# A hybrid of selective scans, additive attention and a graph-gated mixture of experts on one core: norms and keys placed beside other work, a second PSUM place for scores, a larger share for early experts, and gathers paced by small tiles

## The chip, the cores and the metric

One core of one Trainium2 chip runs the whole program in one launch. The metric is the device time in microseconds; below, "us" always means microseconds. Engines are called by their names in the profile: PE (TensorE), PEld (its weight loads), DVE (VectorE), ACT (ScalarE), POOL (GpSimd) and SP (SyncE, which issues nearly all DMAs).

## The reference

The input is `x` of 4 batches x 32 variables x 96 steps x 256 channels. Cut to what matters:

```python
# layer 0: group norm, then two Mamba blocks, one along time, one along the variables
x = x + L0(group_norm(x, 32 groups))
#   in each: xz = x @ in_w.T; depthwise conv of 4 taps; silu; dt, B, C = ...; softplus(dt)
#   h[t] = exp(dt[t] * A) * h[t-1] + dt[t] * B[t] * u[t]     16 states, 512 channels
#   y = (h . C + u * D) * silu(z);  out = y @ out_w.T
# layer 1: t = tokens of x, 4 x 3072 x 256
q, k = ln(t) @ Wt, ln(t) @ Wx                      # 32 features
e = tanh(q[:, :, None] + k[:, None, :] + bh) @ Wa  # every pair of tokens of a batch
t = t + softmax(e) @ ln(t)
# graph attention over 1,048,576 edges (src beyond the 12,288 tokens is clipped, such dst dropped), gives gates
alpha = softmax over the edges of a node of leaky_relu(a_src[src] + a_dst[dst])
scores = layernorm(sum alpha * h[src]).mean(heads);  gates = softmax(top 2 of 4)
t = t + sum over experts of gates * (gelu(ln(t) @ W1[e] + b1[e]) @ W2[e] + b2[e])
```

The tanh of every pair is the largest single piece: 4 x 3072 x 3072 x 32 values.

## The kernel before

The program is written as generators that hand out work in small steps; the order in which they are drawn is the order in which PE, ACT, DVE and POOL execute. Only SP's order is left to the scheduler.

**Layer 0** (`Layer0`) works in 64 blocks of 384 tokens: for each batch eight along time ("t") and eight along the variables ("d"), with the first time block of the next batch ahead of the "d" blocks. A block is 48 slots long; in it `back` runs the scan: decays `dA` on ACT (L385), inputs `dB` (L393) and scans `h` (L402) on DVE, products with `C` on POOL (L409). The rows `bB` and `bC` are broadcast by DMAs of 384 KB, two pairs ahead (L350). `front` prepares the next block (slots 9 to 45). It holds a wide tile with tag `uab`, one buffer, from slot 32. Up to block 16 sums over states are PE products (`lead`), afterwards POOL sums. The group norm of all four batches (`group_norm`, L120 to L132) comes before everything else: per batch and channel half, two loads of 768 KB, six `bn_stats`, then two small PE products that average over the channels of a group, and a root.

**Attention** (`Attention.units`) handles one "column" per round: one ACT tanh of 128 x 3072 (L815), 768 columns a batch. `scores` multiplies it into `pe` in PSUM (L788), eight columns a unit. After the eighth, `unit_tail` takes the maximum on DVE (L877), the exponential on ACT (L884), turns it round (L891) and multiplies by the values (L900). `th` has three buffers, `pe` a single one of two banks, so the products of a unit's first column are held until the exponential of the unit before is under way. Each round advances layer 0 by one slot.

What attention needs beforehand, the norm and projections of a batch (`keys`, some 48 steps), lies in the list `side`; `beside()` draws one step of it per round that has room. If the keys of a batch are missing when its first column is due, rounds go by without a tanh, one step of the keys in each.

**When layer 0 is done**, `Edges.sort` (DVE) compacts the edge lists beside the columns, with a budget of 2.4 us a column; its one-hot products go to PE. When the next-to-last batch is normalised, `Experts.early` computes experts of the finished tokens beside the last batch, as far as a budget allows that grows by `SLOT_US` a column; hidden products `ph` (L1632) are emptied by DVE (L1671), outputs `po` (L1640) also (L1683), and kept in DRAM. POOL fetches the destination rows of edges (`gd`, L1052).

**The tail** (`tail`) is an order written by slots: three slots an expert unit (block of 512 tokens, expert). `some(t)` gives POOL credit of `RATE` gathers a call and has it first read a token (`pace`, L1047) from the tile just computed, either a hidden tile of ACT (`h`, L1714) or an output of DVE (`ko`, L1704). Source rows `gs` (L1337) have four buffers. Group j of twelve edges a partition is scored at slot `G0 + PART*j//2`, spread by DVE (`rh`, L1378) and placed by PE (`pa`, L1388). When a quarter of the edges is placed, its gates are made and the kept outputs of its six blocks are added (L1717) and stored. `ps_h` and `ps_o` rotate by one counter over two pools each.

Of the kernel before, what the change touches and what calls it, by code (L numbers as in the profile page):

```python
# [26 lines left out]
P = 128  # L27
# [8 lines left out]
T = 384  # L36
# [26 lines left out]
FIRST, RATE = 14, 2.75  # L63
G0, PART = 10, 6
KO_BUFS = 2
SLOT_US, PRODUCT_US = 1.2, 0.11
# [8 lines left out]
class Layer0:  # L75
# [8 lines left out]
    def __init__(self, ctx, tc, ident, a, x1):  # L84
# [12 lines left out]
        self.group_norm()  # L97

    def group_norm(self):

        nc, wk, ps, const = self.nc, self.wk, self.ps, self.const
        gavg = const.tile([P, P], F32, tag="gavg", name="gavg")
        nc.sync.dma_start(gavg, self.a["gavg"])
        eps = const.tile([P, 1], F32, tag="eps", name="eps")
        nc.vector.memset(eps, 1e-5)
        self.gm = const.tile([P, KC, B], F32, tag="gm", name="gm")
        self.gr = const.tile([P, KC, B], F32, tag="gr", name="gr")
        HB = TOK // 2
        NB = HB // 512
        for b in range(B):  # L110
            gm = self.gm[:, :, b]
            mv = wk.tile([P, KC, 2], F32, tag="gmv", name="gmv")
            gv = wk.tile([P, KC], F32, tag="gv", name="gv")
            for k in range(KC):
                stats = wk.tile([P, 2, NB, 6], F32, tag="gst", name="gst")
                for i in range(2):
                    xs = wk.tile([P, HB], F32, tag="dt", name="xs", bufs=2)
                    nc.sync.dma_start(xs, self.a["xT"][k * P:(k + 1) * P, b, i * HB:(i + 1) * HB])
                    for j in range(NB):
                        nc.vector.bn_stats(stats[:, i, j, :], xs[:, j * 512:(j + 1) * 512])  # L120
                nc.vector.bn_aggr(mv[:, k, :], stats.rearrange("p i n s -> p (i n s)"))
            pg = ps.tile([P, T], F32, tag="pp", name="pg")
            nc.tensor.matmul(pg[:, :KC], gavg, mv[:, :, 0], start=True, stop=True)
            nc.vector.tensor_copy(gm, pg[:, :KC])

            nc.vector.tensor_tensor(gv, mv[:, :, 0], gm, ALU.subtract)
            nc.vector.tensor_tensor(gv, gv, gv, ALU.mult)
            nc.vector.tensor_tensor(gv, gv, mv[:, :, 1], ALU.add)
            pg2 = ps.tile([P, T], F32, tag="pp", name="pg2")
            nc.tensor.matmul(pg2[:, :KC], gavg, gv, start=True, stop=True)  # L130
            nc.scalar.activation(self.gr[:, :, b], pg2[:, :KC], AF.Sqrt, bias=eps)
        nc.vector.reciprocal(self.gr, self.gr)  # L132
# [419 lines left out]
    def run(self):  # L552
# [34 lines left out]
        for n, blk in enumerate(blocks):  # L587
# [15 lines left out]
            ahead = self.front(then, blk["lead"]) if then and not breaks else {}  # L603
            for slot in range(48):
# [3 lines left out]
                for part in (left[1], jobs[1], ending, ahead):  # L608
# [31 lines left out]
class Attention:  # L640
# [4 lines left out]
    def __init__(self, ctx, tc, ident, a, x1, x2, xn2T, tab_s, tab_a):  # L645
# [7 lines left out]
        self.ps_e = pool("ate", PE_BUFS, space=PSUM)  # L653
# [122 lines left out]
    def units(self, side):  # L776
# [24 lines left out]
        while i < B * PER + LAG or todo or self.later:  # L801
            b, col = self.entry, self.col = divmod(i, PER)
            if b < B and "krep" not in self.state[b]:
# [3 lines left out]
                for f in late:  # L807
                    f()
                yield
# [15 lines left out]
            if behind and i >= LAG:  # L825
                n, k = divmod(i - LAG, NK)
                if k == 0:

                    pe = self.ps_e.tile([P, 2, JB], F32, tag="pe", name="pe")
# [16 lines left out]
            elif todo and hasattr(todo[0], "us"):  # L846
                if not todo[0].full:
                    beside()
                todo.pop(0)()
# [12 lines left out]
            if busy is None:  # L862
                beside()
            i += 1
# [708 lines left out]
class Experts:  # L1573
# [3 lines left out]
    def __init__(self, ctx, tc, x2, xn2T, gates, out, dram, beside=None):  # L1577
# [4 lines left out]
        self.ps_h, self.ps_o = [pool("fp", 2, space=PSUM)], [pool("fo", 1, space=PSUM)]  # L1582
        self.kept, self.done = (beside.kept, beside.units()) if beside else ({}, [])
        self.xts, self.turn = {}, 0

    def open(self, ctx, w):
# [4 lines left out]
        self.ps_h.append(pool("fp2", 2, space=PSUM))  # L1591
        self.ps_o.append(pool("fo2", 1, space=PSUM))

    def bank(self, pools, shape, tag):
        self.turn += 1
        return pools[self.turn % len(pools)].tile(shape, F32, tag=tag, name=tag)
# [133 lines left out]
def tail(tc, a, ed, ex, w, tab_s, tab_a, gates):  # L1730


    with ExitStack() as ctx:
# [376 lines left out]
```

## Time and profile before

| | us |
|---|---|
| median of 3 runs (15323.25 to 15328.89) | 15326.61 |
| the profiled execution's own time | 15328.57 |
| its span, first to last instruction | 15326.8 |
| PE busy | 11744.9 (77%) |
| DVE busy | 11006.6 (72%) |
| ACT busy | 12153.9 (79%) |
| POOL busy | 8997.6 (59%) |
| tanh, L815: 3072 x 2848 ns | 8661.7 |

A share of busy time is an average over stages with different limits; the slices and a table of stretches tell them apart. The first tanh starts at 2565.3 us, the last at 14201.7; all before is layer 0 alone, all after is the tail. A matmul's end is modelled, so a busy PE isn't PE at its peak; the mean granted clock was 0.893.

### The profile page before, as it was taken

The numbers are of one execution on the slowest core, as the hardware profiler recorded it, in microseconds if no ns is written. First come the engines' busy times: TensorE is split into PE (matmuls) and PEld (weight loads), VectorE is DVE, ScalarE is ACT, GpSimd is POOL, SyncE is SP. The second block draws the span as 40 slices with busy tenths as digits, with TensorE's granted clock in tenths as the row PEclk, the third lists the DMA queues.
The fourth block names the chain that finished last, engine by engine and source line by source line (L and its number), as shares of the span: only waits on it lengthen the run. The fifth ranks groups of instructions, "written<-read, shape, count | busy, mean of one in ns | idle before, by whom it ended". The sixth has DMA issues, their size and how long they took to land. (4 is left out here: it accounts for less than half of the span.)

```text
span 15326.8 us, 225317 instructions
## 1 busy us (share of the span) xinstructions
PE 11744.9 (77%) x86496; PEld 5137.0 (34%) x86496; DVE 11006.6 (72%) x15895; ACT 12153.9 (79%) x9327; POOL 8997.6 (59%) x6935
## 2 busy tenths in 40 slices
PE   5666764777777767788887777888876778988997
PEld 2222332222222233333333333333332334433554
DVE  7888888777777887777777877577778864321367
ACT  3443334999999979999999899999997889999221
POOL 4555556777777767767767677477750024400684
PEclk8888887888888888989998889999988989999998
DMA  5666665445445444454454444355531000010234
GB/s 192 204 203 200 198 204 167 149 148 156 152 150 151 158 156 148 150 152 151 151 150 156 147 149 152 110 156 151 154 127 37 24 13 13 10 31 22 66 95 138
DMA packets 1209121, 2007.93 MB, mean 131 GB/s; under 512 B 412384, under 2 KB 655712, under 8 KB 1204960
## 3 DMA queue, kind: packets, MB, share of 16 engines
q1 hardware_dynamic: 1180384, 1988.07, 41.6%
q0 software_dynamic: 27648, 5.36, 0.8%
q8 instruction: 680, 11.14, 0.3%
q14 instruction: 409, 3.35, 0.1%
HBM read 1875.19 MB, written 117.83 MB: 130 GB/s over the span
## 5 line engine op out<-in xcount | busy, mean ns | idle before, releaser
L815 ACT ACTIVATE th<-krep,qsel 128x3072 f32<-128x3072 f32 x3072 | 8661.7, 2848 | 411.1 <-PE pe L788 392.0
L788 PE MATMUL pe<-th,wa_blk 128*32 128x384 f32 x49152 | 4999.3, 535 | 1196.7 <-ACT pr L884 957.3
L409 POOL TENSOR_TENSOR h<-h,bC 128x768 f32<-128x768 f32 x2048 | 3756.2, 1834 | 3000.4 <-DVE h L402 2634.4
L402 DVE TENSOR_TENSOR_SCAN h<-dA,dB 128x384 f32<-128x384 f32 x4096 | 3687.3, 942 | 1109.4 <-ACT dA L385 752.9
L788 PEld LDWEIGHTS pe<-th,wa_blk 128*32 128x32 f32 x49152 | 1448.0, 116 | 3775.6 <-issue 1992.1
L393 DVE TENSOR_TENSOR dB<-bB,dtu 128x768 f32<-128x768 f32 x2048 | 1942.3, 948 | 123.3 <-DMA bB<-bc 91.2
L385 ACT ACTIVATE dA<-dt,t_A 128x380 f32<-128x380 f32 x2048 | 1127.1, 571 | 887.6 <-DVE h L402 883.1
L385 ACT ACTIVATE dA<-dt,d_A 128x372 f32<-128x372 f32 x2048 | 1102.9, 562 | 601.3 <-DVE h L402 595.9
L428 PE MATMUL py<-h,ident 128*128 128x384 f32 x2176 | 1010.1, 597 | 679.6 <-POOL h L409 678.2
L416 POOL TENSOR_TENSOR h<-h 128x768 f32<-128x768 f32 x752 | 1423.0, 1892 | 53.6
L900 PE MATMUL pv<-xn,pT 128*32 128x257 f32 x18432 | 1116.1, 391 | 172.3 <-DVE pT L893 171.4
L959 POOL TENSOR_SCALAR sf<-sel,f 128x32 f32<-128x32 f32 x384 | 148.6, 410 | 1641.6 <-ACT f L955 1533.9
L893 DVE COPY pT<-ptw 128x512 f32<-128x512 f32 (+1 forms) x768 | 419.0, 546 | 703.7 <-PE ptw L891 703.0
L428 PEld LDWEIGHTS py<-h,ident 128*128 128x128 f32 x2176 | 445.4, 223 | 1247.6 <-POOL h L409 1015.2
L900 PEld LDWEIGHTS pv<-xn,pT 128*32 128x32 f32 x18432 | 583.5, 112 | 759.7 <-DVE pT L893 317.4
L417 POOL TENSOR_TENSOR h<-h 128x384 f32<-128x384 f32 x752 | 783.7, 1042 | 59.0
L418 POOL TENSOR_TENSOR y<-y,h 128x384 f32<-128x384 f32 x752 | 779.9, 1037 | 59.0
L1714 ACT ACTIVATE h<-ph,b 128x512 f32<-128x512 f32 x148 | 96.7, 685 | 662.9 <-POOL pace L1047 473.9
L1337 POOL DMA_INDIRECT gs<-tab_s,si x432 | 526.6, 1219 | 131.3 <-issue 98.8
L891 PE MATMUL ptw<-ident,pr 128*128 128x128 f32 x2304 | 484.7, 328 | 143.5 <-DVE pT L893 79.6
L902 DVE COPY pvs<-pv 128x257 f32<-128x257 f32 x384 | 160.2, 417 | 569.0 <-PE pv L900 568.8
L1052 POOL DMA_INDIRECT gd<-tab_a,di x432 | 467.2, 1082 | 140.6 <-issue 133.4
(302 smaller groups left out, 15311.0 us busy)
## 6 DMA issues: line engine op xcount, KB each, us to landing
bB<-bc SPq DMA_DIRECT2D x2048, 384.0 KB
bC<-bc SPq DMA_DIRECT2D x2048, 384.0 KB
all<-kept SPq DMA_DIRECT2D x24, 2048.0 KB
x<-x SPq DMA_DIRECT2D x144, 256.0 KB
kept<-ko SPq DMA_DIRECT2D x59, 512.0 KB
x<-x SPq DMA_DIRECT2D x192, 128.0 KB
xt<-xn2T SPq DMA_DIRECT2D x41, 512.0 KB
qsel<-xn2T SPq DMA_DIRECT2D x75, 256.0 KB
```

The source lines that it names most:

```text
L385: nc.scalar.activation(inner(dA[:, :T]), inner(blk["dt"][:, e, :]), AF.Exp, scale=blk["w"]["A"][:, e, i + s:i + s + 1])
L393: nc.vector.tensor_tensor(dB, blk["bB"].pop(j), z["dtu"].unsqueeze(1).to_broadcast([P, SB, T]), ALU.mult)
L402: nc.vector.tensor_tensor_scan(h[:, s, :], z.pop(("dA", e, i + s))[:, :T], z["dB"][:, s, :], 0.0, ALU.mult, ALU.add)
L409: nc.gpsimd.tensor_tensor(h, h, blk["bC"].pop(j), ALU.mult)
L416: nc.gpsimd.tensor_tensor(h0, h0, h1, ALU.add)
L417: nc.gpsimd.tensor_tensor(h0[:, 0, :], h0[:, 0, :], h0[:, 1, :], ALU.add)
L418: nc.gpsimd.tensor_tensor(y[e], y[e], h0[:, 0, :], ALU.add)
L428: nc.tensor.matmul(z["py"], self.ident, h[:, s, :], start=(i == 0), stop=(i == DS - 1))
L788: nc.tensor.matmul(pe[q * QU:(q + 1) * QU, j, :KQ // 2], self.wa[:, k, :], th[:, c0:c0 + KQ // 2], start=(k == 0), stop=(k == NK - 1))
L815: nc.scalar.activation(th, s["krep"], AF.Tanh, bias=s["qsel"][:, col:col + 1])
L900: nc.tensor.matmul(pv[q * QU:(q + 1) * QU, :C + 1], pT[:, i, q * QU:(q + 1) * QU], s["xn"][:, q * NK + i, :], start=(i == 0), stop=(i == N ...
L1337: nc.gpsimd.indirect_dma_start(out=gs[:, u, :], out_offset=None, in_=rows, in_offset=bass.IndirectOffsetOnAxis(ap=ed.si[:, q, c0 + u:c0 + ...
```

## The change

1. `group_norm(0)` alone stays at the start. The nine remaining steps (two channel halves and the factors, for batches 1 to 3) are handed out by `norm_beside` to blocks 1, 2, 3 and 17 to 22, in the slots 0 to 23. Their data stand in the wide tile, both halves at once.
2. In rounds without keys two steps of `side` are drawn instead of one; likewise in rounds with room, as long as layer 0 is a batch ahead (`asked > b + 1`).
3. When layer 0 is done, a second pool gives a second place for `pe`; units alternate, and nothing is held. For it `ph` of the early experts has one bank instead of two.
4. `SLOT_US` 1.2 to 1.35: 29 early expert units instead of 22, so 30 in the tail instead of 37 (counted in the two programs).
5. In the tail `some` copies a token into a small tile (eight buffers), by ACT after a hidden tile, or sets one to zero on DVE after an output; POOL reads that. `RATE` 2.75 to 3.2, `PART` 6 to 5: 176 tokens are read instead of 209.
6. `bank` counts per tag. The tail has for `ph` one bank and three, for `po` one and one.

```diff
-FIRST, RATE = 14, 2.75
-G0, PART = 10, 6
+FIRST, RATE = 14, 3.2
+G0, PART = 10, 5
-SLOT_US, PRODUCT_US = 1.2, 0.11
+SLOT_US, PRODUCT_US = 1.35, 0.11
...
-        self.group_norm()
+        self.norm_constants()
+        self.group_norm(0)
+        self.norms = [(b, k) for b in range(1, B) for k in range(KC + 1)]
...
+        def load():
+            v["x"] = self.wide("xs")
+            v["st"] = self.wk.tile([P, NB, 6], F32, tag="gst", name="gst")
+            for h in range(2):
+                cols = slice(h * TOK // 2, (h + 1) * TOK // 2)
+                nc.sync.dma_start(v["x"][:, cols], self.a["xT"][k * P:(k + 1) * P, b, cols])
...
+    def norm_beside(self):
+        if not self.norms:
+            return {}
+        b, k = self.norms.pop(0)
+        if k == KC:
+            mean, variance, mean2, root = self.factors(b)
+            return {0: [mean], 1: [variance], 12: [mean2, root]}
+        return {slot: [f] for slot, f in zip((0, 10, 12, 14, 17, 20, 23), self.channel_norm(b, k))}
...
+            norms = self.norm_beside() if n in (1, 2, 3) or n > 2 * NBLK else {}
...
-                for part in (left[1], jobs[1], ending, ahead):
+                for part in (left[1], jobs[1], ending, ahead, norms):
...
+                beside()
                 yield
                 beside()
                 continue
...
-                    pe = self.ps_e.tile([P, 2, JB], F32, tag="pe", name="pe")
+                    places = self.ps_e2 if self.ps_e2 and n // NK % 2 else self.ps_e
+                    pe = places.tile([P, 2, JB], F32, tag="pe", name="pe")
+                if k == 0 and not self.ps_e2:
                     held = behind.pop(0)
...
                     beside()
+                    if self.asked > b + 1:
+                        beside()
...
             if busy is None:
                 beside()
+                if self.asked > b + 1:
+                    beside()
...
-        self.ps_h, self.ps_o = [pool("fp", 2, space=PSUM)], [pool("fo", 1, space=PSUM)]
+        self.ps_h, self.ps_o = [pool("fp", 1, space=PSUM)], [pool("fo", 1, space=PSUM)]
...
-        self.ps_h.append(pool("fp2", 2, space=PSUM))
+        self.ps_h += [pool("fp2", 3, space=PSUM)] * 3
...
     def bank(self, pools, shape, tag):
-        self.turn += 1
-        return pools[self.turn % len(pools)].tile(shape, F32, tag=tag, name=tag)
+        self.turn[tag] = self.turn.get(tag, -1) + 1
+        return pools[self.turn[tag] % len(pools)].tile(shape, F32, tag=tag, name=tag)
...
             credit[0] += RATE
             if credit[0] >= 1:
-                ed.behind(t)
+                tok = gr.wk.tile([P, QU], F32, tag="tok", name="tok", bufs=8)
+                if t is None:
+                    nc.vector.memset(tok, 0.0)
+                else:
+                    nc.scalar.copy(tok, t)
+                ed.behind(tok)
...
-                some(to[n - 1][:, 2 * part - 1, :QU])
+                some()
...
+                att.ps_e2 = actx.enter_context(
+                    tc.tile_pool(name="ate2", bufs=1, side="right", space=PSUM))
```

## The prediction

> **What bounds the kernel now.** I read four views in this order: the page's 40 slices (stages), the table of stretches cut at the stage borders, the waits of one stretch, and the groups of GpSimd in the last one. A slice is 383 us.
>
> ```profile
> PE   5666764777777767788887777888876778988997
> DVE  7888888777777887777777877577778864321367
> ACT  3443334999999979999999899999997889999221
> POOL 4555556777777767767767677477750024400684
> ```
>
> The reader sees three regimes: up to slice 6 ACT is at 3 or 4 and DVE at 8 (layer 0 alone); then ACT at 9 up to slice 37, with dips at 15, 23 and 31 to 33; then the tail, PE and POOL.
>
> ```profile
> core 0: us, PE busy (x) PEld busy (x) DVE busy (x) ACT busy (x) POOL busy (x), PEclk, DMA share, GB/s
> 0.00:62.00 62.00, 4.60 (x16) 4.00 (x16) 36.26 (x83) 3.88 (x7) 0.19 (x4) 1.00 0.79 254
> 62.00:2390.00 2328.00, 1532.86 (x3376) 680.42 (x3376) 1963.82 (x2366) 933.85 (x1637) 1354.55 (x856) 0.85 0.63 200
> 2390.00:2557.00 167.00, 77.09 (x187) 44.28 (x186) 141.46 (x238) 41.87 (x68) 110.33 (x77) 0.64 0.53 164
> 2557.00:5230.00 2673.00, 1977.89 (x17276) 749.89 (x17275) 2078.72 (x2787) 2626.81 (x1987) 2019.72 (x1441) 0.88 0.49 151
> 5490.00:5575.00 85.00, 48.41 (x126) 29.61 (x127) 74.89 (x121) 20.87 (x34) 56.81 (x39) 0.66 0.50 159
> 11760.00:12470.00 710.00, 533.59 (x4768) 211.65 (x4768) 632.98 (x1036) 583.30 (x242) 24.61 (x29) 0.89 0.09 28
> 12470.00:14203.00 1733.00, 1539.17 (x15844) 704.19 (x15840) 545.41 (x1054) 1691.27 (x697) 476.31 (x716) 0.95 0.08 18
> 14286.00:15165.00 879.00, 811.75 (x2403) 468.10 (x2402) 520.69 (x925) 194.74 (x250) 739.47 (x734) 0.96 0.33 85
> ```
>
> In the first 62 us only the group norm runs. In 2390:2557 and 5490:5575 ACT is 25% busy: attention waits for keys, and VectorE (85%, 88%) is what works. In 2557:5230 and 12470:14203 ACT is 98% busy: bound. In 11760:12470 ACT falls to 82% while DVE, sorting edges, is at 89%. In the tail's main stretch PE (92%) and POOL (84%) are both near full.
>
> ```profile
> ACT th L815 <- PE pe L788: 75.9, 47, 6.7
> PE pe L788 <- ACT pr L884: 77.7, 18, 10.3
> ACT pr L884 <- DVE nb L877: 41.5, 13, 7.6
> PE po L1640 <- DVE ko L1683: 25.7, 9, 7.3
> ```
>
> These are waits of 11760:12470: the one score place in PSUM makes PE wait for the exponential, the tanh waits for PE, and the exponential for DVE's maximum.
>
> ```profile
> L1337 POOL DMA_INDIRECT gs<-tab_s,si x422 | 517.1, 1225 | 106.6 <-issue 96.1 <-DVE y L1717 2.3 <-ACT h L1714 1.9
> L1052 POOL DMA_INDIRECT gd<-tab_a,di x104 | 116.8, 1123 | 27.9 <-issue 27.9
> L1047 POOL TENSOR_SCALAR pace<-h 128x32 f32<-128x32 f32 x140 | 66.6, 476 | 3.6
> L1047 POOL TENSOR_SCALAR pace<-ko 128x32 f32<-128x32 f32 x68 | 39.8, 586 | 1.6
> ```
>
> All of POOL in 14286:15165: its idle time is almost only "issue", 0.19 us an instruction. So POOL is full there, and ACT's 473.9 us of waiting for `pace` in the tail is the echo of that.
>
> [...] the trace has 1.283 us loads [...] so 1.28 is used. [...] `gs`, 0.94 us at the shortest and 2.96 while a 2.16 us `rh` of DVE runs; so POOL's mean of 1.2 should stay.
>
> **The parts.** Two counts from the instruction order of both programs (no time is in it): the first tanh comes after 1136 decays instead of 1168, and at the border of batches 0 and 1 8 decays stand between tanhs instead of 26. At four decays in three slots that is 24 and 13.5 slots less without a tanh.
>
> *Norms.* Removed at the start: three of four batches. `gr` is ready at 60.2 now; with batch 0 alone (second channel now waits for the one wide place: statistics end at 10.2, load about 4, six statistics 3.8, two small products and root 3.5) at about 22: -38. Added to blocks 1 to 3: 12 bn_stats x 0.63 + 2 aggregates x 0.32 + small ones = 9 us of DVE, which is at 84% in 62:2390 and sets the pace: +9. Four loads of 768 KB stand in SP's queue ahead of `bB`, `bC`; at the 254 GB/s of the start each is 3.1 us, and the broadcasts are two pairs ahead: +0 to +12, I take 3. Batches 2 and 3 fall in blocks 17 to 22: +6 where keys are made with DVE as bound, else beside an ACT that is full. Three root table loads: +4, counted below. Sum -20 (-38 to 0).
>
> *Keys.* A slot of layer 0 alone is (2190 - 105)/(16 x 48) = 2.7 us; in the keys' stall 208/48 = 4.3. The keys' own work stays, so 24 slots fewer give 24 x 2.9 = -70 (none if waits within a keys step set the 4.3; -104 at full price). Border 0/1: now 48 columns and 19.5 stalled slots from request to next tanh, 283 us; after, 24 and 6, with two steps each, at some 5.5 us: 165. That is -118, but 24 columns at 3.8 had to be done before: +91. So -97 when batch 1 begins. Layer 0 is then 37 slots behind the columns: as many columns run beside it at 3.95 us (mean of batch 2) instead of at 3.01 (1733/576): +35. Sum -62 (-90 to 0). Who is late next: VectorE, at each later border, in fewer columns.
>
> *Second PSUM place against one bank for `ph`.* In 11390:12470 th<-pe costs ACT 60.5 + 75.9 = 136 us; the second place takes away its cause. What it can give is limited by DVE: 633 + 285 busy of 1080, and 2.7 more expert units in these columns add 2.7 x (4 x 0.74 + 2 x 0.68) = 12. Against it, PE now waits at each `ph` for DVE. Nearest row: `po`, with one bank all along, 25.7 us for 12 evictions, 2.1 each; about 42 evictions x 2.1 = 88 us on a PE that is 75% busy and no longer loses its 158 us to `pr`. I take -35 (-100 to +40). In 12470:14203 ACT's th<-pe is 35: -20 at best. Added there: seven more gelus at 1.9 = 13 and 8 + 6 table loads = 18, all on the bound: +31. PE gets 4.6 units x 16.7 = 77 us more, 89% to 93%, and some 70 `ph` waits of 0.4 (po<-ko here: 9.5 us in 23) to 1: +10. Sum of this stage +21 (-10 to +70).
>
> *Tail.* Seven units leave it: 7 x 15 us of PE (ph 273.9 + po 280.9 over 37). But POOL has the same 526 gathers from 14286 on: 526 x 1.205 + 176 tokens x 0.512 + 702 x 0.19 = 857, against 879. So -22, not -105. The units' 119 ACT copies (0.2 us, as the 128x4 exponential) lie on an ACT that is 22% busy; 57 memsets (0.06) on DVE wait for a token place eight back, where DVE now waits for POOL 6.9 us in all: ol, rh, additions and so PE stand behind it: +7. RATE and PART bring more gathers a slot (POOL sooner full) and fewer slots; from POOL's last gather to the last `pa` it is 13 slots instead of 14. Closing blocks unchanged (81 us). Sum -15 (-90 to +20).
>
> Together -20 - 62 - 35 + 21 - 15 = -111. The profiled execution is 15328.6 (span 15326.8), 2 above the median of the three runs: 15328.6 - 111 = 15217.6, so about **15216** as a median.
>
> **Rivals.** *The tail follows PE.* PE at 92% speaks for it; if POOL gets room, the tail gives -105 instead of -15: 15126. *Denser keys buy nothing*: DVE is 85% busy in the stall, slots grow in proportion, the stall lasts as long; -62 becomes 0: 15278. *Slower: the lone `ph` bank.* If each of some 110 evictions holds PE behind the sort's instructions and tanh follows PE, the experts' larger share makes PE the bound from 11760 on: the second place gives nothing (0 for -35), 110 x 2.1 = 231 come instead of 21: 15216 + 35 + 210 = 15461. With the second place giving nothing, the gain is gone at (111 - 35 + 21)/110 = 0.9 us an eviction that reaches ACT, and above 1.2 the kernel is slower. Against it: three th buffers and 158 us of PE wait that go away. *The places do not alternate*, or `ph` serializes before them: H stays as it is, 15250.
>
> **How the numbers follow.** Forecast 0.60, tail by PE 0.16, keys nothing 0.14, `ph` bound 0.10 (a part of it under the full price). Errors of the parts together are about 85 around 15216; the range 15110 to 15310 leaves out most of the last rival and a little at the lower end. About 0.2% (31 us) is what a measurement of this kernel can tell from no change. Faster by more: nearly all of the first two, most of the third: 0.85. Same 0.06, slower 0.09.
>
> **What would show it.** Right: first decay at about 70 instead of 105; first tanh some 100 us sooner; next border's gap near 30 us instead of 85; no PE pe <- ACT pr in the last batch; some PE ph <- DVE h; POOL still without idle time in the tail, ending some 20 us sooner by its own length. Wrong: POOL idle in the tail (PE bound, larger gain); a last batch with more than 3.1 us a column (`ph`); bB waits in blocks 1 and 2 of more than 12 us.

## The result: slower by 60 us, where a gain of 111 had been forecast

| | before | after |
|---|---|---|
| median of 6 runs each, us | 15325.19 (15322.06 to 15328.89) | 15384.85 (15371.01 to 15396.19) |
| ratio, with its 95% interval | | 1.0037 [1.0027, 1.0048] |
| profiled execution, us (span) | 15328.57 (15326.8) | 15383.73 (15381.5) |

The forecast was 15216, and its range ended at 15310. Landmarks below are read from the traces, each of a single execution; where the medians say more, they are given. The page of the changed kernel has these slices:

```profile
PE   5666765677777767888888677888876779988886
DVE  8888887777777777777777877577767873332367
ACT  3443436999999979999999799999996879999221
POOL 5555556777777657767777577476750014410684
```

The stages have kept their places. ACT's dip at the second border is still there (slice 23), and DVE is at 7 and 8 in slices 31 to 33, where edges are sorted. The table of stretches of the changed kernel, with the columns of the table shown before:

```profile
0.00:26.00 26.00, 3.63 (x8) 2.18 (x8) 10.87 (x30) 3.09 (x4) 0.19 (x4) 1.00 0.78 242
26.00:2356.00 2330.00, 1515.09 (x3369) 673.26 (x3368) 1966.93 (x2379) 934.58 (x1634) 1347.82 (x852) 0.86 0.63 201
2356.00:2477.00 121.00, 65.13 (x176) 40.02 (x176) 92.17 (x187) 21.11 (x36) 54.08 (x37) 0.70 0.42 133
2477.00:5163.00 2686.00, 2003.04 (x17268) 755.72 (x17268) 2097.53 (x2792) 2634.81 (x1986) 2005.79 (x1435) 0.86 0.49 151
5465.00:5517.00 52.00, 29.73 (x90) 17.10 (x94) 34.84 (x67) 9.67 (x14) 20.95 (x15) 0.61 0.35 114
11741.00:12695.00 954.00, 733.76 (x6576) 306.66 (x6576) 785.30 (x1242) 782.26 (x323) 64.89 (x91) 0.91 0.09 29
12695.00:14250.00 1555.00, 1402.59 (x14342) 662.13 (x14338) 510.64 (x984) 1516.10 (x629) 434.57 (x654) 0.97 0.09 22
14330.00:15218.00 888.00, 775.78 (x2243) 435.74 (x2244) 531.22 (x985) 214.71 (x358) 730.69 (x700) 0.94 0.31 80
```

The group norm's start has shrunk (first row), the keys' stall is 121 us where it was 167, and the gap where batch 1 begins is 52 where it was 85. So the first third gained. In 11741:12695, the columns 2304 to 2560, ACT and DVE are both at 82%. The same columns of the kernel before:

```profile
11761.00:12660.00 899.00, 704.03 (x6566) 293.34 (x6566) 695.30 (x1153) 766.83 (x316) 117.09 (x165) 0.90 0.08 24
```

There ACT was at 85% and DVE at 77%. DVE does 90 us more in these columns now, and it is the sort: its instructions take 636 us there instead of 540. Layer 0's last decay came 90 us later (at 11467.9 instead of 11378.1 us), the sort begins only when layer 0 is done, and so more of it falls into these columns.

To see where the gain went, each piece between two landmarks (starts of layer 0's first decay and of the columns' tanhs) is compared:

| stretch | before, us | after, us | difference |
|---|---|---|---|
| start to first decay | 105.2 | 67.3 | -38 |
| first decay to first tanh | 2460.1 | 2410.0 | -50 |
| first tanh to column 768 (batch 1) | 3008.7 | 3039.9 | +31 |
| 768 to 1408 | 2596.7 | 2560.1 | -37 |
| 1408 to 1536 (keys of batch 2) | 543.6 | 578.8 | +35 |
| 1536 to 2304 | 3046.7 | 3084.6 | +38 |
| 2304 to 2560 (edges sorted) | 899.4 | 954.7 | +55 |
| 2560 to last tanh, 3071 | 1541.3 | 1554.3 | +13 |
| last tanh to end | 1125.1 | 1131.8 | +7 |

The sum is +55 (rounded terms give 54). 88 us are saved up to the first tanh, and 143 net come back behind it. Landmarks of runs with identical code up to there differ by up to 26 us (the run with tokens, whose code differs in the tail alone, stood 14 us ahead at the first tanh and 24 at the last). Their stretches behind the first tanh agree within about 10 us, so the difference of a stretch is worth more than one landmark.

The waits of 11741:12695 in the changed kernel (us in total, times, longest):

```profile
ACT th L860 <- PE pe L832: 113.7, 71, 7.1
PE ph L1684 <- DVE h L1723: 68.1, 36, 11.5
PE pe L832 <- ACT pr L936: 52.5, 16, 9.6
ACT pr L936 <- DVE nb L929: 40.8, 19, 9.2
PE po L1692 <- DVE ko L1735: 28.9, 11, 8.6
```

`pe` still waits for `pr`, which two alternating places should have ended, and the wait for the one `ph` bank is new: 1.9 us for each of 36. GpSimd's groups in 14330:15218 of the changed kernel:

```profile
L1389 POOL DMA_INDIRECT gs<-tab_s,si x420 | 528.3, 1258 | 109.4 <-issue 105.7 <-DVE tok L1817 1.7 <-DVE oh L1426 0.6
L1104 POOL DMA_INDIRECT gd<-tab_a,di x104 | 126.7, 1218 | 28.2 <-issue 27.9 <-ACT h L1766 0.3
L1099 POOL TENSOR_SCALAR pace<-tok 128x32 f32<-128x32 f32 x175 | 77.8, 445 | 14.2 <-ACT h L1766 9.9
```

POOL is as full as before: busy for 82% of this stretch (84% before), and 133.6 us of its idle time are "issue". It reads 33 tokens fewer, but each gather takes longer (1258 and 1218 ns against 1225 and 1123).

### The profile page after: what moved, and what is told of

Same layout as the page of the kernel before. It is cut to its first block, busy times and chain, and to the rows that moved or that the text cites. A ratio compares the mean times of both kernels' runs of the same rounds, so it can differ in the third digit from the quotient of the medians.

```text
span 15381.5 us, 225571 instructions
## 1 busy us (share of the span) xinstructions
PE 11765.2 (76%) x86496; PEld 5132.3 (33%) x86496; DVE 11066.4 (72%) x15983; ACT 12192.1 (79%) x9436; POOL 8977.4 (58%) x6902
## 4 chain that ended last, share of the span: by engine, by line
ACT 36%; PE 22%; DVE 19%; issue 9%; POOL 9%; DMA 4%; another core or an unknown queue 0%; SPq 0%; DVEq 0%; POOLq 0%; ACTq 0%
ACT th L860 26%; PE pe L832 9%; ACT dA L427 5%; DVE h L444 5%; PE pv L952 4%; POOL h L451 3%; DVE dB L435 2%; POOL gs L1389 2%; DMA bB<-bc 2%; ACT pr L936 1%; PE pz L501 1%; PE po L1692 1%; PE ptw L943 1%; PE ex L1598 1%; PE ph L1684 1%
## 5 line engine op out<-in xcount | busy, mean ns | idle before, releaser
L929 DVE TENSOR_REDUCE nb<-pe 128x1 f32<-128x768 f32 x384 | 362.9, 945 | 361.0 <-PE pe L832 359.6
```

## The experiments

They come in the order of the reasoning. "Before" in a comparison is the kernel before, measured beside it on the same chip. A gap is the time from the start of one tanh to the start of the next; a tanh takes 2.8 us, so a gap of 2.7 is none.

### One part alone: norms with the tail's edits

```diff
+        self.norm_constants()
+        self.group_norm(0)
+        self.norms = [(b, k) for b in range(1, B) for k in range(KC + 1)]
...
-FIRST, RATE = 14, 2.75
-G0, PART = 10, 6
+FIRST, RATE = 14, 3.2
+G0, PART = 10, 5
...
+                tok = gr.wk.tile([P, QU], F32, tag="tok", name="tok", bufs=8)
...
+        self.turn[tag] = self.turn.get(tag, -1) + 1
```

> The kernel before with two parts of the change: the norms handed out beside the blocks, and the tail's tokens, RATE, PART and rotation by tag (37 units stay in the tail). Both theories see the norms as the change's trace has them: first tanh 30 us sooner. Theory 'norms kept': the 30 us stay in every later column, since ACT is full. Theory 'norms lost': their later loads and statistics come back at the borders, 0 to -15 by the last batch. Tail: if POOL is the bound, the stretch from last tanh to end falls by about 20 us (fewer tokens) from 1125; if PE is, it stays within 10 us of 1125. Whole: 15275 (kept, POOL) to 15320 (lost, PE).

Measured: 15327.45 against 15328.58, ratio 0.9998 [0.9990, 1.0007]. The first decay came 37.6 us earlier and the last tanh 28.5 earlier: the norms keep most of what they save. The tail took 1152.0 us instead of 1125.1 and used it up.

### One part alone: both denser steps of the keys

```diff
+                beside()
                 yield
                 beside()
                 continue
...
+                    if self.asked > b + 1:
+                        beside()
...
+                if self.asked > b + 1:
+                    beside()
```

> The kernel before with the denser steps of the keys alone, in stalls and in columns. Theory 'borders give it back': first tanh 55 us sooner, and of this 20 to 35 us are lost at each later border, where two steps a column make VectorE and PE wait for each other, so that the last batch begins between 20 us sooner and 40 us later; whole 15310 to 15365. Theory 'keys are a gain' (the prediction's): the last batch begins 40 us or more sooner; whole 15265 or less, and then the loss of the change lies in the last batch alone.

Measured: 15360.97, ratio 1.0022 [1.0013, 1.0030], slower. The first tanh came 57.5 us earlier, column 768 36.8, column 1536 44.5, column 2304 10.5; the last tanh came 18.0 later. The traced execution is 13 us below the median; by the medians the keys cost 32 us. So the keys' part alone turns its gain into a loss.

### One part alone: the second place, with one bank for `ph`

```diff
+                    places = self.ps_e2 if self.ps_e2 and n // NK % 2 else self.ps_e
+                    pe = places.tile([P, 2, JB], F32, tag="pe", name="pe")
+                if k == 0 and not self.ps_e2:
...
+        self.ps_h, self.ps_o = [pool("fp", 1, space=PSUM)], [pool("fo", 1, space=PSUM)]
```

> The kernel before with the second place of the scores alone, and for it one bank for ph in the early experts (share 1.2 stays). Nothing differs before column 2212. Theory 'lone bank': PE waits for VectorE at ph (some 60 us in the sort's columns), the place gains less than that: columns 2212 to 3071 take 20 to 60 us more, whole 15345 to 15385. Theory 'place gains' (the prediction's): 20 to 60 us less, whole 15265 to 15305.

Measured: 15358.82, ratio 1.0020 [1.0011, 1.0029], slower. Columns 2304 to 2560 took 14 us longer, the rest to the last tanh 11, the tail 14. (In the tail of this run `ph` has one bank and three in turn, where it had two and two.)

### The changed kernel with the smaller share

```diff
-SLOT_US, PRODUCT_US = 1.35, 0.11
+SLOT_US, PRODUCT_US = 1.2, 0.11
```

> The changed kernel with SLOT_US back at 1.2: the larger share undone, all else as changed. Theory 'share is the loss': the last batch (tanh 2304 to 3071) falls by 25 us or more, and the tail, bound by POOL, grows by less than 15 although seven units return to it: whole 15345 to 15370. Theory 'share is even or a gain': last batch 5 to 20 us less, tail 30 to 60 more: whole 15390 to 15425.

Measured: 15389.01 against 15328.58, ratio 1.0040 [1.0026, 1.0055], no different from the changed kernel. Its last tanh stood 23.7 us earlier than there, its tail took 1153.7 us instead of 1131.8. Seven expert units cost the last batch what the tail saves.

Taken one by one, these four account for the whole: by their medians the first three runs differ from the kernel before by -1, +32 and +30 us and the share by nothing, 61 together, where the change cost 60. Of the 55 us that columns 2304 to 2560 lost, the keys alone bring 18, the place with one bank 14 and the share 19.

### The two keys' steps apart

In the keys' stall only:

```diff
+                beside()
                 yield
                 beside()
                 continue
```

> The kernel before with two steps of the keys a round in rounds without a tanh only; in columns one, as before. First tanh 57 us sooner, as with both. Theory 'pairing' (two steps beside a tanh make VectorE and PE wait for each other): most of it stays, the last tanh comes 25 us or more sooner, whole 15290 to 15305. Theory 'offset' (whatever starts the columns sooner leaves as many of layer 0's slots to run beside columns at 4 us, and stalls come at each border): the last tanh within 15 us of before, whole 15315 to 15345.

In the columns only:

```diff
+                    if self.asked > b + 1:
+                        beside()
...
+                if self.asked > b + 1:
+                    beside()
```

> The kernel before with two steps of the keys in columns only, while layer 0 is a batch ahead; stalls as before. First tanh unchanged. Theory 'pairing': each later border costs 20 to 40 us, the last tanh comes 20 us or more later, whole 15345 to 15380. Theory 'offset': the border of batches 0 and 1 stalls for about 6 slots less, and the last tanh stays within 15 us, whole 15315 to 15345.

Measured: the stall alone 15380.66 against 15318.97, ratio 1.0042 [1.0025, 1.0059]; the columns alone 15284.79, ratio 0.9979 [0.9970, 0.9987]. With the stall alone the first tanh came 66 us earlier, the gap at batch 1 grew from 84.5 to 108.0 us, one of 71.3 appeared at batch 2, and the last tanh was 60 us late. With the columns alone the gap at batch 1 was 2.7 us and the last tanh 34 us early. Both results lie outside what either theory allowed. By their medians the two, +62 and -34, nearly add up to the +32 of both steps.

That gave what I call the lead theory: in stalled rounds layer 0 advances by a slot too, and its lead over the columns hides the next keys. It is half of the truth, as the two runs with empty rounds will show.

### The place with shared banks, and tokens alone

```diff
-        self.ps_h, self.ps_o = [pool("fp", 2, space=PSUM)], [pool("fo", 1, space=PSUM)]
+        self.ps_h = self.ps_o = [pool("fp", 2, space=PSUM)]
```

> As e3_place (second place of the scores, share 1.2), but the early experts' ph and po share two banks in turn, so ph no longer waits for its own eviction. Theory 'lone bank': the last batch takes 20 us or more less than in e3_place, last tanh at or before that of the kernel before. Theory 'place' (the second place itself does not pay, since VectorE sets the sort's columns and the exponential waits for its maximum anyway): last tanh within 10 us of e3_place, that is 10 to 30 us later than before.

```diff
+                tok = gr.wk.tile([P, QU], F32, tag="tok", name="tok", bufs=8)
+                if t is None:
+                    nc.vector.memset(tok, 0.0)
+                else:
+                    nc.scalar.copy(tok, t)
+                ed.behind(tok)
```

> The kernel before with the small token tiles alone; RATE 2.75, PART 6 and the common rotation stay. Nothing differs before the tail. Theory 'tokens couple': eight tokens tie ACT and VectorE closer to POOL, PE falls behind, last tanh to end 1140 us or more (1125 before, 1152 with RATE and PART too). Theory 'RATE and PART': the 27 us come from fewer calls a gather, which leave more units behind POOL's last gather; here 1115 to 1130. POOL's stretch from first to last gather stays 918 us within 10 in both.

Measured: 15316.96, ratio 1.0000 [0.9993, 1.0007], and 15324.41, ratio 1.0005 [0.9996, 1.0013]. With shared banks the loss in columns 2304 to 2560 fell from 14 to 4 us and the tail took 1115 us instead of 1140: the lone bank costs. But behind column 2560 the loss stayed (14 us, 11 with the lone bank), and the place itself gave nothing. TensorE's waits in 12640:14130 of this run tell why:

```profile
PE pe L788 <- ACT pr L885: 138.8, 45, 11.2
```

That is the wait of a single place, in a kernel with two. `n` in `n // NK % 2` is already the quotient by `NK`, so it counts units: eight units go to one place, then eight to the other.

### The place chosen anew for each unit

```diff
-                    places = self.ps_e2 if self.ps_e2 and n // NK % 2 else self.ps_e
+                    places = self.ps_e2 if self.ps_e2 and n % 2 else self.ps_e
```

In the kernel with shared banks:

> The run with the second place and shared banks for the experts' sums, with one edit: the place is chosen by n % 2 in place of n // NK % 2. n counts units of score sums already, so the change's expression keeps eight units in one place and then eight in the other. If that is why the last batch gained nothing, TensorE's waits for the softmax's exponentials (149 us, 49 times there, 141 us, 53 times in the kernel before) go to under 20 us, and the stretch from the first tanh of batch 3 to the last tanh is 15 to 60 us shorter: 15255 to 15300 us. If the wait only hides one for the DVE or ACT behind it, the waits move (to the probabilities' transpose or to tanh) and the time stays within 15 us of 15317.

Measured: 15250.41 against 15320.15, ratio 0.9957 [0.9940, 0.9973], faster. TensorE's waits in the same stretch are now

```profile
PE ptw L892 <- ACT pr L885: 77.7, 44, 8.5
PE pe L788 <- ACT th L815: 55.9, 99, 5.1
```

and none of `pe` for `pr`. The rows of 12640:14130 in the table of stretches, first with blocks of eight units, then alternating:

```profile
12640.00:14130.00 1490.00, 1308.91 (x13468) 601.04 (x13460) 468.68 (x915) 1443.65 (x596) 379.43 (x578) 0.94 0.08 19
```

```profile
12640.00:14130.00 1490.00, 1330.16 (x13844) 608.56 (x13840) 476.15 (x920) 1481.36 (x614) 376.82 (x567) 0.97 0.08 19
```

ACT was busy 96.9% and is now busy 99.4%; a column takes 2.95 us instead of 3.04. ACT's own wait for `pe` was 40.9 us there and is 6.4. From column 2304 to the last tanh this is 53.4 us less than before, against 17.7 more with blocks of eight.

The same edit in the changed kernel itself:

> The changed kernel with one edit: the place for the score sums is chosen by n % 2 in place of n // NK % 2. In the kernel with shared banks the same edit took the stretch from the first tanh of batch 3 to the last tanh from 17.7 us over the kernel before to 53.4 us under it, so 71 us. Here the hidden rows have one bank and DVE's emptying of it stays, and seven more units are computed beside the last batch, so 40 to 70 us are expected: 15310 to 15340 us, TensorE's waits for the exponentials in the last batch under 20 us. If the lone bank bounds the last batch, less than 20 us comes: 15360 to 15385.

Measured: 15345.24 against 15325.89, ratio 1.0015 [1.0008, 1.0022]: 40 us under the changed kernel, and `pe` waits no more for `pr` in its last batch. `ph` still waits for DVE there, 18.5 us. The expression was worth about 40 us here, and is not all.

### Norms and columns together, and the stall's step undone

The kernel before with the norms and the columns' steps:

```diff
+            norms = self.norm_beside() if n in (1, 2, 3) or n > 2 * NBLK else {}
...
+                    if self.asked > b + 1:
+                        beside()
```

> The kernel before with two of the parts: the norms of batches 1 to 3 beside layer 0, and the denser step in the columns only (the rounds in which the attention waits for keys keep one step). Places, tail, shares as before. The lead theory (layer 0's lead over the columns is what hides the next keys, and the stall's rounds spend it while a column's does not) has the two gains add: the norms alone moved the last tanh 28.5 us forward, the columns' step 34.4 us, and the tail stays at 1123 to 1126 us. It expects 15255 to 15270 us, no gap over 10 us where batch 1 begins. If instead the norms' DVE work in blocks 1 to 3 and a denser layer 0 compete, the sum is less than the columns alone gave (15285) or even.

Measured: 15262.26 against 15320.15, ratio 0.9961 [0.9947, 0.9975]. The two add up, 28.5 and 34.4 alone, 64 at the last tanh together.

The changed kernel with a single step in the stall's rounds:

```diff
                     f()
-                beside()
                 yield
                 beside()
                 continue
```

> The changed kernel with one edit: the stall's rounds go back to one step of layer 0; the columns keep two. The lead theory: the first tanh comes some 55 us later than in the changed kernel, the gap where batch 1 begins falls from 51 to under 10 us, and the last tanh and the end come 50 to 60 us earlier than in the changed kernel: 15325 to 15340 us. The rival that two steps per column are what costs (DVE and PE in each other's way): the first tanh is late and nothing comes back, 15385 to 15440 us.

Measured: 15299.06, ratio 0.9986 [0.9979, 0.9993]. Against the changed kernel the first tanh came 50 us later; at column 768 the two were within 3 us; at 1408 this one was 35 ahead, at 2304 60, at the last tanh 67. With each measured against the kernel before beside it, it gained 81 us where 50 to 60 were expected. The lead explains that the 50 us are made up at column 768 (gap 2.7 instead of 51.3 us). It doesn't explain columns 768 to 1408, where nothing stalls.

### Where a block of layer 0 begins in a unit of attention

Looking there, I ordered the runs by us a column between 768 and 1408. Lead doesn't order them: the changed kernel, with the smallest (2168 decays done at column 768), takes 4.00 us, the columns' steps alone (2192) 3.94, the kernel before (2218) 4.06. Something else differs. A block has 48 slots, a unit eight columns, and each column draws one slot; so a block's first decay falls at the same column of a unit for hundreds of columns, and only rounds without a tanh (or without a slot) move it. In this stretch the traces show it at about 1.7 before, at 7.7 in the changed kernel, at 4.7 with the columns' steps (0 is a unit's first column). I call this place the alignment. Rounds that advance layer 0 alone change it, and otherwise only put layer 0 a few slots further ahead:

```diff
-        i = 0
+        i, empty = 0, 5
...
-            if b < B and "krep" not in self.state[b]:
-
+            if b < B and ("krep" not in self.state[b] or b == 1 and empty):
+                ready = "krep" in self.state[b]
+                empty -= ready
                 yield
...
-                beside()
+                if not ready:
+                    beside()
                 continue
```

In the kernel before, five such rounds:

> The kernel before with five rounds put in where batch 1 begins, after its keys are ready, in which layer 0 advances by a slot and nothing else is drawn. A block of layer 0 has 48 slots, a unit of attention eight columns, and a column takes one slot, so a block begins at the same column of a unit for hundreds of columns: in the kernel before at 1.7 (columns 768 to 1791), with the columns' denser steps at 4.7. Five slots move it from 1.7 to 4.7. If the place in the unit sets the rate (the alignment theory), the five rounds cost some 22 us at column 768, and columns 768 to 1408 then take 3.94 us each instead of 4.06: 77 us less, and columns 1536 to 1792 3.89 instead of 3.99 (25 us less); the end comes 50 to 80 us earlier, less 20 us in columns 1856 to 2176 (4.02 instead of 3.97): 15250 to 15300 us. If the rate comes from how far layer 0 is ahead or from the keys' steps, it stays at 4.06, and layer 0 is five slots further: 15320 to 15345 us.

Measured: 15264.60 against 15315.69, ratio 0.9965 [0.9952, 0.9977]. Five rounds of idling attention make the kernel before faster by 51 us. The stretch 768 to 1408, first before, then with the five rounds:

```profile
5574.00:8171.00 2597.00, 2082.05 (x16936) 885.57 (x16932) 1950.34 (x2759) 2465.84 (x1844) 1826.58 (x1310) 0.90 0.49 150
```

```profile
5572.00:8095.00 2523.00, 2039.70 (x16946) 877.62 (x16950) 1971.78 (x2761) 2462.17 (x1844) 1828.24 (x1315) 0.91 0.50 155
```

The instruction counts are the same on every engine within 18, ACT's busy time within 4 us, and 74 us are gone: ACT goes from 94.9% to 97.6% busy. What ACT waits for in these stretches, before and then with the five rounds:

```profile
ACT th L815 <- PE pe L788: 84.3, 62, 4.7
ACT dA L385 <- DVE h L402: 32.0, 51, 2.9
```

```profile
ACT th L817 <- PE pe L788: 25.5, 44, 2.7
ACT dA L385 <- DVE h L402: 21.2, 33, 3.0
```

59 of the 74 us are tanhs that waited for a `th` buffer because the score sums were late, 11 are decays that waited for the scan. A rate of 3.941 us a column was reached where 3.94 was expected.

In the changed kernel, three:

> The changed kernel with three such rounds at the same place; they move the start of a block from 7.7 to 4.7 of a unit in columns 768 to 1408, and from 6.7 to 3.7 after column 1536. The alignment theory: some 13 us more at column 768, 4.00 to 3.94 us a column up to 1408 (38 us less), then 3.89 to 4.01 in columns 1536 to 1792 (30 us more) and 4.03 to 4.05 in 1856 to 2176 (7 us more): 15385 to 15400 us at the end, a gain that is given back. If only the lead counts, three slots more of it: rates unchanged, 15380 to 15400 at the end. The rates by stretch tell the two apart, not the end.

Measured: 15330.64 against 15315.69, ratio 1.0009 [1.0001, 1.0018]. The changed kernel lay 60 us above its kernel before, this one lies 15 above: a gain of 45, where none was expected at the end. The same stretch, first as changed, then with the three rounds:

```profile
5517.00:8077.00 2560.00, 2068.82 (x16848) 877.86 (x16836) 1969.87 (x2735) 2454.50 (x1836) 1821.15 (x1307) 0.91 0.49 151
```

```profile
5524.00:8034.00 2510.00, 2014.77 (x16832) 867.99 (x16836) 1962.73 (x2730) 2449.02 (x1832) 1825.92 (x1307) 0.91 0.50 154
```

The rate went from 4.00 to 3.92. That also rules the lead out: at the same place, 4.7, the two runs with empty rounds take 3.94 us with 2224 decays done at column 768 and 3.92 with 2172, where the kernels they start from take 4.06 with 2218 and 4.00 with 2168. Why the score sums are less late at 4.7 than at the other places seen here wasn't looked into. The expectation for the later columns was wrong in one point: the slot that moves the changed kernel's place by one at batch 2 fell away, so the place stayed at 4.7 and, after layer 0's skip near column 1800, at 1.7 (not 3.7 and 0.7), and the gain was kept.

This run has the same places as the one with the stall's step undone, so the two compare that step without the alignment. It is 55 us ahead of that run at the first tanh and 2 to 4 us behind it at columns 768, 1536 and 2304 (its three rounds made the gap at batch 1 some 10 us longer). Then it falls 18 us behind by the last tanh, with layer 0 done 52 us later; by the medians (1.0009 against 0.9986) the whole is some 36 us slower. So doubling the steps in the stall is worth 55 us up to the first tanh, nothing at column 768, and is a loss at the end. And the run with five rounds (single steps) has the places of the one with the columns' steps: there the doubled steps cost 38 us more between 1408 and 1536, 37 between 2176 and 2304 and 15 between 2304 and 2560, against 11 us for the five rounds' longer gap and some 21 gained at the first border. By the medians the run with five rounds is also 17 us further under its kernel before (51 against 34). So the 34 us of the columns' steps came from the alignment that they brought; at equal alignment the steps cost time.

### The tail's parts, and the parts joined

```diff
-FIRST, RATE = 14, 2.75
-G0, PART = 10, 6
+FIRST, RATE = 14, 3.2
+G0, PART = 10, 5
```

> The kernel before with two numbers of its tail: RATE 3.2 instead of 2.75 gathers per call and PART 5 instead of 6. Tokens, rotation of the PSUM banks and all else as before. The norms' run had a tail of 1152 us from its last tanh against 1125 before, and tokens alone 1128. If the numbers are the cause, the tail here is 1145 to 1155 and the time 15345 to 15355 us; if the rotation by tag (with a third bank less for the hidden rows of the first part) is, the tail stays at 1120 to 1130 us and the time at 15325.

The first experiment's norms and tail, with one counter for the pools:

```diff
-        self.turn[tag] = self.turn.get(tag, -1) + 1
-        return pools[self.turn[tag] % len(pools)].tile(shape, F32, tag=tag, name=tag)
+        self.turn += 1
+        return pools[self.turn % len(pools)].tile(shape, F32, tag=tag, name=tag)
```

> The run with norms and the tail's edits, with the one counter of the kernel before for the PSUM pools instead of one by tag. That run's tail took 1152 us from the last tanh; tokens alone 1128, RATE and PART alone 1131. If counting by tag is the cause, the tail here is 1125 to 1135 us and the time 15300 to 15310; if tokens and the two numbers only cost together, it stays at 1145 to 1155 us and 15325.

Measured: 15323.78, ratio 1.0001 [0.9993, 1.0010], tail 1130.8 us; and 15318.89, ratio 0.9995 [0.9986, 1.0004], tail 1145.8. With tokens alone it was 1127.9. So neither cause named for the first experiment's 27 us holds alone: the numbers and the tokens cost only together. (In the traces, tails of the same code differ by up to 12 us: 1118 to 1127 in the kernel before's, 1120 to 1132 in the changed kernel's. The 21 and 27 us of both together are beyond that, single steps between these runs are not.) With 37 units in the tail the numbers let POOL finish sooner but leave the last expert units behind: the last hidden tile came 987 us after the last tanh before, 1058 with the numbers, 1072 with tokens as well, 1079 with the count by tag besides. With 30 units, as in the changed kernel, it came at 942 and POOL's edges ended the tail. Why tokens delay the units once the numbers are changed wasn't settled.

The norms, the columns' steps, the alternating place and shared banks on the kernel before:

> The kernel before with the norms of batches 1 to 3 beside layer 0, the denser step in the columns only, the alternating second place (n % 2) and banks shared by the experts' sums; tail and share as before. By the single runs: norms and columns together 58 us (15262), place 70 us (15250); their stretches lie apart (before and after layer 0's end), so they add: 15185 to 15200 us. If the place's gain came from work that the later keys left over, the sum is smaller: 15210 to 15240.

And the same with the share and the tail's two numbers:

```diff
-SLOT_US, PRODUCT_US = 1.2, 0.11
+SLOT_US, PRODUCT_US = 1.35, 0.11
...
-FIRST, RATE = 14, 2.75
-G0, PART = 10, 6
+FIRST, RATE = 14, 3.2
+G0, PART = 10, 5
```

> The run with norms, columns' steps and alternating place joined, and SLOT_US 1.35, RATE 3.2, PART 5 besides; tokens are not copied and the banks are counted together as before. RATE and PART alone ended the edges' products 24 us nearer to the last tanh, but the last expert units then ended the tail; with 30 units in place of 37 these end earlier. With alternation the last batch has room, so the seven early units cost less than the 24 us they cost in the changed kernel. Expected 15165 to 15190 us; if the last batch pays for the units in full, 15190 to 15215.

Measured: 15194.13 against 15325.89, ratio 0.9914 [0.9898, 0.9931]; and 15211.99, ratio 0.9923 [0.9907, 0.9940]. The first, 132 us faster than the kernel before, is the best version that ran; it is the sum of its parts (58 and 70). The second has a tail of 1095 us instead of 1117 and a stretch from column 2304 to the last tanh that is 31 us longer. Its 15212 is what was expected if the last batch pays for the units in full. The share moves work and saves none. The five rounds in place of the columns' steps, with the rest of the best version, weren't tried.

## Why the prediction was wrong, by its own steps

Forecast and result lie 171 us apart. By the medians of the single runs the keys were off by 94 us (-62 forecast, +32 measured) and the second place by 65 (-35, +30); the norms with the tail's edits by 34 (-35, -1). The +21 of the last batch stood against them.

**Norms (-20): right.** The first decay came at 67.3 us where about 70 was named, and 28.5 us are kept at the last tanh (38.5 in the other run with the same norms and tail's edits, with one counter).

**Keys (-62): wrong sign.** The step that failed is "So -97 when batch 1 begins": the keys alone stood at -37 there. That run shows its three terms. "24 x 2.9 = -70" was of the right kind and too large: 57 us (42 to 66 in the traces with this step, 1.8 to 2.8 a slot). The border, "-118", gave 94: it took 285 us before, from the request for batch 1's keys (at column 720) to column 768, and 191 us with the denser steps (request at column 744). And the 24 columns more before that, "+91", took 115. A gap near 30 us had been named and in the changed kernel it was 51. The lead was counted as so many slots to be made up later at 0.94 us (+35), and not as what the first border draws on at once: with the stall's step alone the gap grew from 84.5 to 108.0 us. The next term was named without a price, "VectorE, at each later border, in fewer columns": it is 37 us at each of the second and third borders at equal alignment. And the alignment had no term at all: the table of stretches averages over a unit, so 4.06, 4.00 and 3.94 us a column looked like one number. The empty rounds moved 74 and 50 us with it in the one stretch of columns 768 to 1408, as much as the largest part of the change was to bring. The rival "denser keys buy nothing" came nearer in size, but not by its reason: the stall did get shorter.

**Second place (-35 in the sort's columns): the rival "the places do not alternate" is what happened.** The forecast read `n // NK % 2` as an alternation by units. The mechanism behind it was right: alternating, with two shared banks kept, it gives 19 us in columns 2304 to 2560 and 34 in the rest of the last batch. That is 53 together, where -35 and "-20 at best" stood, so the sum was sized well and the second half of it too small. The rival had the right cause and the wrong price: it put the place at nothing, but without a gain the lone `ph` bank remained, 14 us in columns 2304 to 2560 and some 24 in the tail when compared with shared banks. Its wait was sized well, 1.9 us for 2.1, 36 times for 42.

**Last batch (+21): near the number, not by its terms.** From column 2560 it was +13 us and 3.04 us a column, under the 3.1 named as a warning, and the lone bank didn't bound it. But the place, which was to give up to 20 us here, cost 11 when it was alone, and the share, put at +31, cost 5 here and 19 in columns 2304 to 2560. That these errors nearly cancel is luck. Where the places do alternate, the share costs 31 us from column 2304 on (the two joined runs), the size that was forecast.

**Tail (-15): +7 in this trace.** Three other runs with the same tail took 1119.5 us (the stall's step undone), 1119.7 (alternating places) and 1122.9 (three empty rounds) where 1125.1 had been before, so it stayed about even. Two effects stand against each other in it: with 37 units the tail's edits had added 27 us (1125.1 to 1152.0), and the seven units less took 22 off again (1153.7 to 1131.8). That POOL bounds the tail fits: the last hidden tile came 45 us earlier than before, and the tail hardly ended sooner. So the rival that the tail follows PE falls for this kernel; with 37 units and the new numbers the expert units do come last. The term that was mis-sized is POOL's sum, which kept the gathers at 1.205 us, their mean before; that it would stay was an estimate, and 1.250 was measured. POOL's busy time for tokens fell by 29 us (106.4 to 77.8), but 420 `gs` took 33 ns more each (14 us) and 104 `gd` 95 ns more (10), and POOL waited 14.2 us for tokens where it had waited 5.2. From the start of the first `gs` to that of the last gather it was 926.2 us, and 914.8 to 920.8 in the three other runs, against 917.6 before: not down by 22. The two numbers without the tokens do shorten it, to 904.3 us with 37 units and 898.1 with 30 (the second joined run); there the `gs` took a mean of 1165 and 1170 ns, in four runs with both 1246 to 1275. Of the gathers in the tail's main stretch (14286:15165 before, 14330:15218 after) 125 of 525 ran beside an `rh` of DVE in the trace of the kernel before and took a mean of 1.86 us, the others 1.00; in the trace of the changed kernel it was 150 of 524, with 1.90 and 0.99 us. So what grew is mainly how many of them coincide with an `rh`; why the tokens go with that is open.

## What to carry to other kernels

When two periodic programs are interleaved step by step (48 slots here, eight columns there), any edit that adds or removes a round shifts one against the other, until another such round shifts them again. Before a difference is put down to the edit, compare runs with equal alignment, or move the alignment alone; a few empty rounds may be worth more than the edit. Time saved before a stage begins is not yet saved: ask what used to be done in the idle rounds (here layer 0's lead), and who draws on it first. An edit that should end a wait is tested by looking for that wait in the trace: the second place showed in one line that it wasn't used.

## What the runs showed of the hardware

Only timings that had been taken for constants. Gathers of the same rows took a mean of 1165 to 1275 ns (`gs`) and 1123 to 1281 ns (`gd`) in different runs of the tail. In the traces of the kernel before and the changed one, those that ran beside an `rh` of DVE (2.2 us) took 1.86 and 1.90 us, the others 1.00 and 0.99; for the other runs this isn't shown. The granted TensorE clock in 12640:14130 was 0.94 with the score place changing every eight units and 0.97 with every unit (0.95 in the kernel before), each in one execution; from the first to the second, PE ran 2.8% more instructions there in 1.6% more busy time.
